# New step costs, hand-over time, array-mode charge and ranks in the planner of a pre-norm attention and slot block

## The chip, the cores and the metric

The kernel runs on one core of a Trainium2 chip, in fp32. The metric is the device time of one execution in microseconds (us): the median of three runs is 686.89, from 686.75 to 687.0. The profile shows one further execution of 686.6 us from the first to the last instruction.

The engines are named as in the profile: PE is TensorE (matmuls; PEld its weight loads), DVE is VectorE, ACT is ScalarE, POOL is GpSimd, SP the queue that issues most of the DMAs. Each engine works through its own queue in the order in which the kernel emitted its instructions; a waiting instruction holds up all behind it on that engine.

## What is computed

For 32 sequences of 512 tokens of width 256 two residual sublayers follow each other:

```
x = x + attn(layernorm(x))
    q     = tanh(x Wc + bc)                      charge, one number a token
    shell = normalised(x Ws + bs)                64 wide
    proj  = shell omega + bias; phi_s = [cos, sin](proj)
    tp    = q**m (m = 0..4)  outer  phi_s        5 x 64
    phi   = tp W_combine                         64 wide
    attn  = softmax(causal(phi phi^T * decay / temp));  out = (attn V) W_out
x = x + slots(layernorm(x))
    h     = gelu([x, mean slot] w1 + b1);  route = (h w2 + b2) / tau
    alpha = softmax over the 8 largest of 64 routes
    gi    = (alpha^T x) / sum(alpha);  S = GRU(gi, S0)
    out   = alpha (S wv + bv) wo
```

## The kernel before

**Groups.** Two sequences (GB = 2, 1,024 tokens, 8 tiles of 128) make a group, so there are 16 groups, g = 0 to 15. Every group goes through the same steps; several groups are under way at once. Names in the program carry the group: pf_3_0 is the projection of tile 0 of group 3.

**One group on PE**, in the order in which data passes, with the name that the profile gives the result and its line:

- pf (L971): a token tile times the fused weights, 128x321. DVE scales it to sv (L984). The transposed tokens xT come by DVE (L941) from blocks that DMAs bring (xb), and in groups 0 and 1 from PE (pta, L919).
- ptq (L1030) and pts (L1101): transposes of the charges (POOL's qrep L1010) and shells (POOL's sq L1057 and rn L1077, DVE's shn L1085); pp (L1118): shells times omega; DVE's turn (L1142), ACT's sine (L1150, with a table load), DVE's products tp (L1164); pph (L1176): tp times W_combine; DVE's phi (L1191).
- pl (L1233): logits; DVE's lg (L1262), ACT's exponential pr (L1274); ptp (L1311): transposes of pr, which ACT copies to prT (L1329); po (L1317): prT times V; DVE adds it to x (L1346). This is done for row tiles (0, 1), 2 and 3 and for both sequences.
- POOL's lnb (L1386), ACT's squares xm (L1398), POOL's deviations (L1412 to L1414), ACT's xm (L1428; DVE in the last two groups, L1424). SP writes xm to DRAM (xd) and reads it back in blocks (xmb), which DVE transposes; in the last two groups PE transposes (ptb, L849) and ACT copies.
- ph (L1458): hidden layer; ACT's gelu h_t (L1467, with a table load); prr (L1481): routes; ACT's rlT (L1495); prt (L1487): transpose; ACT's rl (L1504); DVE's top (L1512), ACT's exponential (L1530), DVE's sums, and alpha al (L1546, POOL; DVE in the last two groups); psi (L1570): alpha^T x.
- pt_gi (L1594), giT (ACT, L1602); prz and pn (L1623): gates; DVE, ACT and POOL steps of the GRU; pt_hn (L1594), hnT (ACT); pv (L1745); DVE's val (L1753); py (L1767): alpha times values; ACT copies it to ys (L1780) and POOL issues an accumulating store (L1807).

**Array modes.** A matmul uses all 128 rows and columns of the array or a part. In the code a PE step carries a split: none for the whole array (pf, po, ph, prz, pn, pv and all transposes), "64x64" for pp and pph, "64x128" for pl and py, "128x64" for prr and psi. The profile shows it as 128*128, 64*64, 64*128 or 128*64.

**Setup.** Weights are folded before group 0: wv times W_out (pw0, pb0), the slot layer's values (pw1, pb1, L452 and L484), the mean slot (pt_hs, pb1 L742), the constant part of the gates (pgh, L775). A bias bv1 is loaded by SP and spread over a tile by DVE (L475).

**The planner.** Nothing is emitted while the steps are described: `add(engine, cost, emit, after, uses, ...)` records a step with its cost in us, what it waits for and which buffers it uses. `Plan.order` then plays the program through, and the steps are emitted in the order in which it placed them. It keeps for each engine the time at which it becomes free, for each kind of buffer the times at which its slots come free, and takes again and again the step with the smallest key (earliest time t at which it can start, rank). A result reaches another engine HOP us after its step's cost. The rank of a step is made of its group times STRIDE, its earliest time within the group, and DELAY of its stage, a pair: the first number counts always, the second times max(0, g - last + 3), that is in the last groups only. A step that would change PE's split has SWITCH added to its rank; no time is charged for the change.

Of the kernel before, what the change touches and what calls it, by code (L numbers as in the profile page):

```python
# [15 lines left out]
P = 128  # L16
# [61 lines left out]
HOP = 0.5  # L78
TABLE = 1.28
SWITCH = 0.23  # L80
STRIDE = 22.39
# [3 lines left out]
    "setup": (0.0, 0.0),  # L85
    "load": (22.2, -11.2),
    "tokens": (0.1, -0.9),
    "angles": (-39.5, -3.6),
    "phi": (-8.7, 0.0),
    "weights": (12.9, -3.8),  # L90
    "values": (-6.4, -1.5),
    "normal": (10.0, -1.9),
    "router": (-0.7, 1.2),
    "taken": (-2.6, 1.8),
    "gru": (28.9, -1.7),
    "given": (43.1, 8.2),
# [25 lines left out]
class Plan:  # L122
# [32 lines left out]
    def order(self):  # L155
# [34 lines left out]
        for n, s in enumerate(self.steps):  # L190
            s.n = n
            if not s.waits:
                ready[s.eng].append(s)
        placed = []
        while len(placed) < len(self.steps):
            best = None
            for e, todo in ready.items():
                for s in todo:
                    t = max(free[e], s.ready)
                    need = {}  # L200
                    ok = True
                    for u in s.uses:
                        if not u.live and u.tag in slots:
                            need[u.tag] = need.get(u.tag, 0) + 1
                    for tag, k in need.items():
                        if len(slots[tag]) < k + (s.spare if tag == "ps" else 0):
                            ok = False
                            break
                        t = max(t, heapq.nsmallest(k, slots[tag])[-1])
                    if not ok:  # L210
                        continue
                    if s.table and s.table != table:
                        key = (t + TABLE, s.rank + TABLE, s.n)
                    elif e == "PE" and s.split != split:
                        key = (t, s.rank + SWITCH, s.n)
                    else:
                        key = (t, s.rank, s.n)
                    if best is None or key < best[0]:
                        best = (key, s, t)
            assert best is not None, "no step can be placed"  # L220
            _, s, t = best
            ready[s.eng].remove(s)
            if s.table and s.table != table:
                t, table = t + TABLE, s.table
            if s.eng == "PE":
                split = s.split
            for u in s.uses:
                if not u.live:
                    u.live = True
                    if u.tag in slots:  # L230
                        heapq.heappop(slots[u.tag])
            s.start, end = t, t + s.cost
            free[s.eng] = end
            for u in s.uses:
                u.left -= 1
                u.end = max(u.end, end + s.land)
                if not u.left and u.tag in slots:
                    heapq.heappush(slots[u.tag], u.end + HOP)
            for o in s.next:
                o.ready = max(o.ready, end + s.land + (HOP if o.eng != s.eng else 0.0))  # L240
                o.waits -= 1
                if not o.waits:
                    ready[o.eng].append(o)
            placed.append(s)
# [4 lines left out]
def block_kernel(ctx: ExitStack, tc: tile.TileContext, a: dict, out: bass.AP):  # L249
# [554 lines left out]
    def statistics(g, src, uses, after):  # L804
# [6 lines left out]
                0.37,  # L811
# [19 lines left out]
        s = add("POOL", 3.3, spread, ss + [s_ones], [st, ts])  # L831
        return ts, s

    def normalised(g, xm, after):
# [4 lines left out]
        for bb in range(GB):  # L839
# [3 lines left out]
            if g >= NG - LAST_BY_TENSOR:  # L843
                for k in range(KD):
                    pt = bank(f"ptb_{g}_{bb}_{k}")

                    def turn(bb=bb, k=k, pt=pt):
                        for c in range(NT):
                            nc.tensor.transpose(  # L849
                                pt()[:, c * P : (c + 1) * P],  # L850
                                xm()[:, bb * NT + c, k * P : (k + 1) * P],
                                ident,
                            )

                    s = add("PE", 0.47, turn, of + [s_ident], [xm, pt, dst])
                    done.append(
                        add(
                            "ACT",
                            0.54,
                            lambda k=k, dst=dst, pt=pt: nc.scalar.copy(dst()[:, k, :], pt()),  # L860
                            [s],
                            [pt, dst],
                        )
                    )
            else:
# [23 lines left out]
                for h in range(2):  # L889
# [12 lines left out]
                    done.append(add("DVE", 0.63, turn, s_b, [xb, dst]))  # L902
# [3 lines left out]
    def columns(g, xt):  # L906
# [3 lines left out]
        for bb in range(GB):  # L910
            dst = lazy("xT", f"xT_{g}_{bb}", [P, KD, T])
            done = []
            if g < BY_TENSOR:
                for k in range(KD):
                    pt = bank(f"pta_{g}_{bb}_{k}")

                    def turn(bb=bb, k=k, pt=pt):
                        for c in range(NT):
# [6 lines left out]
                    s = add("PE", 0.44, turn, [x_in[g][bb], s_ident], [xt, pt, dst])  # L925
# [3 lines left out]
                            0.54,  # L929
# [6 lines left out]
            else:  # L936
                for h in range(2):
# [12 lines left out]
                    done.append([add("DVE", 0.63, turn, xb_in[g, bb], [xbs[g, bb], dst])])  # L950
# [3 lines left out]
    def features(g):  # L954
# [9 lines left out]
        for t in range(GT):  # L964
# [4 lines left out]
            def project(c=c, pf=pf, tile_=tile_):  # L969
                for k in range(KD):  # L970
# [8 lines left out]
            s = add("PE", 1.1, project, done[c // 2] + w_done, [tile_, pf, sv])  # L979
# [3 lines left out]
                    0.42,  # L983
# [44 lines left out]
        def charges_turned():  # L1028
# [7 lines left out]
        s = add("PE", 0.45, charges_turned, s_rep + [s_ident], [qrep, ptq, qs])  # L1036
        s = add(
            "ACT",
            0.61,
# [7 lines left out]
            0.62,  # L1047
# [22 lines left out]
            0.62,  # L1070
# [5 lines left out]
        def norms():  # L1076
# [3 lines left out]
        s_rn = add("POOL", 2.05, norms, [s], [rn])  # L1080
# [3 lines left out]
                0.35,  # L1084
# [20 lines left out]
        s = add("PE", 0.44, shells_turned, s_shn, [shn, pts, sh_t])  # L1105
        s = add("ACT", 0.54, lambda: nc.scalar.copy(sh_t(), pts()), [s], [pts, sh_t])
# [6 lines left out]
        def projected():  # L1113
            for h in range(2):
# [11 lines left out]
        s = add("PE", 0.55, projected, [s, s_om], pps + [sh_t, ang], split="64x64")  # L1126
# [3 lines left out]
                0.41,  # L1130
# [9 lines left out]
        def nearest():  # L1140
# [8 lines left out]
                0.63,  # L1149
# [7 lines left out]
        for m in (1, 3):  # L1157
# [8 lines left out]
            s_tp.append(add("DVE", 1.25, powers, [s_tp[-1], s_q], [tp, qs]))  # L1166
# [4 lines left out]
        def combined():  # L1171
            for m in range(ORDER + 1):
# [12 lines left out]
            "PE", 2.3, combined, s_tp + [s_wc], phs + [tp, phi], split="64x64"  # L1185
# [4 lines left out]
                0.35,  # L1190
# [14 lines left out]
    def attention(g, sv, s_sv, phi, s_phi):  # L1205
# [11 lines left out]
        for tiles in ((0, 1), (2,), (3,)):  # L1217
# [7 lines left out]
            def logits(tiles=tiles, off=off, pls=pls):  # L1225
# [17 lines left out]
                0.15 + width * 0.00167,  # L1243
# [8 lines left out]
            for bb in range(GB):  # L1252
# [3 lines left out]
                for i in tiles:  # L1256
# [16 lines left out]
                    def weights(bb=bb, i=i, c=c, lg=lg, nm=nm, pr=pr, den=den, tiles=tiles):  # L1273
# [10 lines left out]
                        "DVE", 0.11 + 0.12 * (i + 1), lowest, [s_pl, s_mask], [pls[bb], lg, nm]  # L1284
# [4 lines left out]
                            0.31 + 0.105 * (i + 1),  # L1289
# [8 lines left out]
                0.16,  # L1298
# [5 lines left out]
            for bb in range(GB):  # L1304
# [8 lines left out]
                def values(bb=bb, tiles=tiles, off=off, po=po, pr_t=pr_t):  # L1313
# [11 lines left out]
                s = add("PE", 0.119 * width / P, turned, s_ex[bb], [prs[bb], pt, pr_t])  # L1325
                s = add(
                    "ACT",
                    0.18 + 0.09 * width / P,
# [8 lines left out]
                    0.436 * width / P,  # L1337
# [4 lines left out]
                for d, i in enumerate(tiles):  # L1342
# [13 lines left out]
                    s_x[t] = add("DVE", 0.5, added, [s_po, s_den], [po, den, xt, ln])  # L1356
# [17 lines left out]
    def router(g, s_x, ln):  # L1374
# [6 lines left out]
        for tiles in ((0, 1), (2,), (3,)):  # L1381
# [10 lines left out]
            for bb in range(GB):  # L1392
                for i in tiles:
# [3 lines left out]
                            0.6,  # L1397
# [22 lines left out]
        def moved(t):  # L1420
# [6 lines left out]
            else:  # L1427
# [7 lines left out]
                0.25 if by_vector else 0.51,  # L1435
# [15 lines left out]
        for bb in range(GB):  # L1451
# [4 lines left out]
            def hidden(ph=ph, dst=dst):  # L1456
                for k in range(KD):
# [4 lines left out]
            s = add("PE", 1.78, hidden, done + w1_done, [dst, ph, h_t])  # L1462
# [3 lines left out]
                    0.6,  # L1466
# [18 lines left out]
        def routes_turned():  # L1485
# [5 lines left out]
        s = add("PE", 1.01, route, s_h + [l_w2], h_ts + [prr, rl_t], split="128x64")  # L1491
        s = add(
            "ACT",
            0.6,
# [4 lines left out]
        s = add("PE", 0.44, routes_turned, [s], [rl_t, prt, rl])  # L1499
# [3 lines left out]
            0.54,  # L1503
# [5 lines left out]
        for t in range(GT):  # L1509
# [5 lines left out]
            s_top.append(add("DVE", 0.43, taken, [s], [rl, rest, top]))  # L1515
# [4 lines left out]
            0.62,  # L1520
# [8 lines left out]
            0.68,  # L1529
# [6 lines left out]
        def sums():  # L1536
# [4 lines left out]
        s = add("DVE", 1.53, sums, [s], [rl, rest, asum])  # L1541
# [3 lines left out]
                0.7 if by_vector else 1.1,  # L1545
# [12 lines left out]
    def slots(g, xm, al, s_al, stored):  # L1558
# [19 lines left out]
        def amounts():  # L1578
# [3 lines left out]
        s_psi = add("PE", 1.87, taken_in, s_al, [psi, al, xm, gi], split="128x64")  # L1582
        s_gi = add(
            "ACT", 0.38, lambda: nc.scalar.copy(gi(), psi()[:, 0:D]), [s_psi], [psi, gi]
        )
        s_rw = add("DVE", 0.3, amounts, [s_psi], [psi, rw])

        def halves(n, src, s_src):
# [3 lines left out]
            def turn():  # L1592
# [5 lines left out]
            s = add("PE", 0.22, turn, [s_src], [src, pt, dst])  # L1598
            s = add(
                "ACT",  # L1600
                0.38,
# [9 lines left out]
        side, cost = ("DVE", 0.42) if by_vector else ("POOL", 0.73)  # L1611
# [9 lines left out]
        def gates(dst, lo, n):  # L1621
# [9 lines left out]
        s_rz = add("PE", 1.81, lambda: gates(prz, 0, 2 * D), [s] + W_GRU, [gi_t, prz, rz])  # L1631
        s_n = add("PE", 0.86, lambda: gates(pn, 2 * D, D), [s] + W_GRU, [gi_t, pn, nn])
        s = add(
            "DVE",
            0.75,
# [6 lines left out]
            0.6,  # L1642
# [7 lines left out]
            0.42,  # L1650
# [8 lines left out]
            0.38,  # L1659
# [13 lines left out]
        s_nn = add("ACT", 0.42, lambda: nc.scalar.activation(nn(), nn(), AF.Tanh), [s], [nn], "exp")  # L1673
# [12 lines left out]
        s = add("DVE", 0.94, new_state, [s], [rz, rh, nn, hn])  # L1686
# [4 lines left out]
        if g >= NG - LAST_BY_TENSOR:  # L1691
# [10 lines left out]
            s_a = add("PE", 0.58, weights_turned, s_al, [al, pta, al_t])  # L1702
            s_alt = add("ACT", 0.54, lambda: nc.scalar.copy(al_t(), pta()), [s_a], [pta, al_t])
# [39 lines left out]
        def slot_values():  # L1743
# [5 lines left out]
        s = add("PE", 0.86, slot_values, [s] + s_wov, [hn_t, pv, val])  # L1749
        s_val = add(  # L1750
            "DVE",
            0.38,
# [6 lines left out]
        for c2 in range(NT // 2):  # L1759
# [15 lines left out]
            s = add("PE", 0.95, given, [s_val, s_alt], pys + ys + [al_t, val], split="64x128")  # L1775
            for bb in range(GB):
                if stored:
# [6 lines left out]
                    s_ys[bb].append(add("ACT", 0.54, kept, [s], [pys[bb], ys[bb]]))  # L1784
# [17 lines left out]
                s_y = add("DVE", 0.65, added, [s], [pys[bb], xt])  # L1802
# [90 lines left out]
```

## Time and profile before

| | |
|---|---|
| median of 3 runs | 686.89 us |
| profiled execution, span | 686.6 us |
| DVE, ACT, POOL busy | 553.0, 472.2, 253.8 us |
| DMA of the hardware queue q1 | 89.42 MB |
| mean rate of DMA | 153 GB/s |
| costliest PE rows | po 151.1 us, pf 126.1 us, ph 52.0 us |

A row of the profile gives start and duration of an instruction, or of several alike that follow each other (x8), and in brackets how long its engine stood idle before it and what ended the wait. The duration of a matmul runs until its results are out, and the next matmul starts before that; what a step costs PE is therefore read as the distance from its start to the next start. "x" counts matmul records; in fp32 a matmul of the program appears as two records, a transpose as one.

### The profile page before, as it was taken

Reading aid. Unit: us, or ns where it says so; the run is one execution under the profiler, and the core shown is the slowest. Engines: PE = TensorE matmul, PEld = TensorE weight load, DVE = VectorE, ACT = ScalarE, POOL = GpSimd, SP = SyncE. Lnnn points to the kernel's source line nnn. Section 1 sums busy time; section 2 is a strip of 40 time slices with the busy share of each in tenths; the row PEclk is TensorE's granted clock in tenths of the full one; section 3 lists DMA queues with packets and bytes.
Section 4 is the critical chain, followed back from the end, with each engine's and each line's share of the span. In section 5 each row is a group of like instructions: output and inputs, shape, how many; then the busy total and the mean of one; then the engine's idle time right before and its main releaser. Section 6 shows DMA issues by size and latency. Waiting matters only on the chain.

```text
span 686.6 us, 12389 instructions
## 1 busy us (share of the span) xinstructions
PE 658.0 (96%) x3890; PEld 450.4 (66%) x3890; DVE 553.0 (81%) x1770; ACT 472.2 (69%) x1105; POOL 253.8 (37%) x432
## 2 busy tenths in 40 slices
PE   6968999999999999999999999999999999999985
PEld 5646775667666766767666676757666676677553
DVE  5879788989796979979696987879798877877575
ACT  2227777768677777859677785877768686787651
POOL 6420542143525363242535343335334324322221
PEclk9989999999999999999999999999999999999999
DMA  6674377576567596686778594687768518341447
GB/s 186 182 196 121 116 218 189 121 200 132 170 147 154 164 235 176 153 194 144 174 174 183 171 228 131 130 206 174 163 179 168 157 34 184 78 62 32 62 62 184
DMA packets 225362, 105.30 MB, mean 153 GB/s; under 512 B 153360, under 2 KB 224464, under 8 KB 225296
## 3 DMA queue, kind: packets, MB, share of 16 engines
q1 hardware_dynamic: 209344, 89.42, 48.8%
q0 software_dynamic: 15120, 14.98, 15.1%
q8 instruction: 31, 0.51, 0.3%
q14 instruction: 35, 0.29, 0.1%
q10 hardware_dynamic: 832, 0.10, 0.1%
HBM read 54.34 MB, written 49.81 MB: 152 GB/s over the span
## 4 chain that ended last, share of the span: by engine, by line
PE 81%; DVE 5%; DMA 5%; ACT 4%; SPq 2%; issue 1%; POOL 0%; DVEq 0%; ACTq 0%; POOLq 0%
PE po L1317 20%; PE pf L971 16%; PE ph L1458 7%; PE ptp L1311 5%; PE pl L1233 5%; PE pph L1176 4%; PE py L1767 4%; PE psi L1570 4%; PE prz L1623 4%; DMA x<-in_x_dram 2%; SPq L283 2%; PE prr L1481 2%; PE pv L1745 2%; PE pn L1623 2%; PE pp L1118 1%; DMA bv<-in_bv_dram 1%
## 5 line engine op out<-in xcount | busy, mean ns | idle before, releaser
L1317 PE MATMUL po<-sv,prT 128*128 128x256 f32 x640 | 151.1, 381 | 0.7 <-ACT prT L1329 0.7
L1317 PEld LDWEIGHTS po<-sv,prT 128*128 128x128 f32 x640 | 116.0, 189 | 21.4 <-issue 2.9
L971 PE MATMUL pf<-wfb,xT 128*128 128x321 f32 x448 | 126.1, 434 | 0.0
L971 PEld LDWEIGHTS pf<-wfb,xT 128*128 128x128 f32 x448 | 83.6, 190 | 38.3 <-issue 5.3
L984 DVE SCALAR_TENSOR_TENSOR sv<-pf,lna,bias_f 128x321 f32<-128x321 f32 x128 | 64.1, 541 | 17.1 <-PE pf L971 16.9
L1274 ACT ACTIVATE pr<-lg,nm 128x128 f32<-128x128 f32 (+3 forms) x128 | 70.9, 557 | 9.3 <-DVE nm L1262 9.0
L1346 DVE SCALAR_TENSOR_TENSOR x<-po,den,x 128x256 f32<-128x256 f32 x128 | 57.8, 475 | 20.4 <-PE po L1317 19.1
L1398 ACT ACTIVATE xm<-x,lnb 128x256 f32<-128x256 f32 x128 | 63.9, 506 | 8.9 <-POOL lnb L1386 8.5
L1262 DVE CUSTOM_DVE_ANT_0 lg<-pl,mask 128x128 f32<-128x128 f32 (+3 forms) x128 | 56.6, 481 | 6.7 <-PE pl L1233 6.7
L1010 POOL COPY qrep<-sv 128x128 f32<-128x128 f32 x64 | 17.8, 294 | 118.2 <-DVE sv L984 118.2
L1386 POOL TENSOR_SCALAR lnb<-lnb 128x2 f32<-128x2 f32 (+1 forms) x48 | 18.9, 393 | 114.3 <-DVE x L1346 68.8
L1428 ACT ACTIVATE xm<-x,lnb 128x256 f32<-128x256 f32 x112 | 57.3, 590 | 4.3 <-POOL lnb L1414 4.0
L1329 ACT COPY prT<-ptp 128x384 f32<-128x384 f32 (+1 forms) x96 | 46.8, 519 | 18.3 <-PE ptp L1311 17.3
L1807 POOL DMA_DIRECT2D out_dram<-ys x28 | 38.0, 1508 | 47.0 <-ACT ys L1780 45.9
L1458 PE MATMUL ph<-xmT,w1b 128*128 128x512 f32 x112 | 52.0, 595 | 0.5 <-ACT giT L1602 0.5
L812 DVE BATCH_NORM_STATS2 bna<-x 128x6 f32<-128x256 f32 x128 | 46.3, 409 | 1.8 <-DMA x<-in_x_dram 1.8
L1311 PE MATMUL ptp<-ident,pr 128*128 128x128 f32 x320 | 47.1, 278 | 0.2 <-ACT pr L1274 0.2
L1233 PE MATMUL pl<-phi 64*128 64x256 f32 (+1 forms) x384 | 45.2, 361 | 1.3 <-DVE phi L1191 1.3
L1311 PEld LDWEIGHTS ptp<-ident,pr 128*128 128x128 f32 x320 | 36.3, 140 | 15.1 <-ACT pr L1274 4.3
L1164 DVE TENSOR_TENSOR tp<-tp,qs 128x1024 f32<-128x1024 f32 x32 | 39.2, 1226 | 3.5 <-ACT tp L1150 2.8
L1191 DVE TENSOR_TENSOR phi<-pph,dec_q 128x256 f32<-128x256 f32 x32 | 13.4, 418 | 34.7 <-PE pph L1176 34.7
L1233 PEld LDWEIGHTS pl<-phi 64*128 64x128 f32 x384 | 30.8, 186 | 13.3 <-issue 6.5
(178 smaller groups left out, 1309.8 us busy)
## 6 DMA issues: line engine op xcount, KB each, us to landing
x<-in_x_dram SPq DMA_DIRECT2D x32, 512.0 KB, 6.1
xb<-in_x_dram SPq DMA_DIRECT2D x112, 128.0 KB, 3.3
out_dram<-x SPq DMA_DIRECT2D x28, 512.0 KB, 3.7
xd<-xm SPq DMA_DIRECT2D x28, 512.0 KB, 3.3
xmb<-xd SPq DMA_DIRECT2D x112, 128.0 KB, 2.9
out_dram<-ys POOLq DMA_DIRECT2D x28, 512.0 KB, 7.3
ad<-al SPq DMA_DIRECT2D x14, 256.0 KB, 2.4
ab<-ad SPq DMA_DIRECT2D x56, 64.0 KB, 2.7
```

What stands on the lines that cost most here:

```text
L971: nc.tensor.matmul(pf()[:, 0:NF], tile_()[:, k, c * P : (c + 1) * P], w[:, k, :], start=(k == 0), stop=(k == KD - 1),)
L984: lambda t=t, pf=pf: nc.vector.scalar_tensor_tensor(sv()[:, t, :], pf()[:, 0:NF], ln()[:, 1, t : t + 1], bias_f, ALU.mult, ALU.add,),
L1233: nc.tensor.matmul(pls[bb]()[:, off[i] + lo : off[i] + lo + w], phi()[r, 0, q : q + P], phi()[r, 1, k : k + w], start=True, stop=True,)
L1262: nc.vector.tensor_tensor_reduce(out=lg()[:, c], in0=pls[bb]()[:, c], in1=mask[:, T - w : T], scale=1.0, scalar=TOP, op0=ALU.add, op1=ALU.min,
L1274: nc.scalar.activation(pr()[:, c], lg()[:, c], AF.Exp, bias=nm(), scale=-1.0, accum_out=den()[:, tiles.index(i), bb : bb + 1],)
L1311: nc.tensor.transpose(pt()[:, j : j + P], prs[bb]()[:, j : j + P], ident)
L1317: nc.tensor.matmul(po()[:, d * D : (d + 1) * D], pr_t()[:, lo : lo + P], sv()[:, bb * NT + j, C_V:NF], start=(j == 0), stop=(j == i),)
L1329: lambda width=width, pt=pt, pr_t=pr_t: nc.scalar.copy(pr_t()[:, 0:width], pt()[:, 0:width]),
L1346: nc.vector.scalar_tensor_tensor(xt()[:, t, :], po()[:, d * D : (d + 1) * D], den()[:, d, bb : bb + 1], xt()[:, t, :], ALU.mult, ALU.add, ...
L1398: lambda bb=bb, i=i: nc.scalar.activation(xm()[:, bb * NT + i, 0:D], xt()[:, bb * NT + i, :], AF.Square, bias=ln()[:, 2, bb, i : i + 1], a ...
L1428: nc.scalar.activation(xm()[:, t, 0:D], xt()[:, t, :], AF.Identity, bias=bias, scale=scale)
L1458: nc.tensor.matmul(ph(), w1[:, k, :], dst()[:, k, :], start=(k == 0), stop=(k == KD - 1))
```

## The change

Only numbers in the planner and one rule are changed; no step is added, removed or computed differently, and the buffers are the same.

- HOP goes from 0.5 to 0.3.
- A change of PE's split is charged in time: DRAIN 0.094 plus a FILL that depends on the mode entered. Transposes get a split of their own, "turn", which counts as whole array: between None and "turn" nothing is charged.
- SWITCH, the rank added to a step that would change the mode, goes from 0.23 to 1.828.
- STRIDE goes from 22.39 to 22.714, and all pairs of DELAY are new.
- Nearly every cost handed to `add` is new.

```diff
-HOP = 0.5
+HOP = 0.3
+DRAIN = 0.094
+FILL = {None: 0.107, "turn": 0.055, "64x64": 0.054, "128x64": 0.054, "64x128": 0.107}
 TABLE = 1.28
-SWITCH = 0.23
-STRIDE = 22.39
+SWITCH = 1.828
+STRIDE = 22.714
...
-    "load": (22.2, -11.2),
+    "load": (586.66, 41.42),
...
-    "angles": (-39.5, -3.6),
-    "phi": (-8.7, 0.0),
+    "angles": (-254.44, -137.72),
+    "phi": (-94.38, -95.74),
...
-    "given": (43.1, 8.2),
+    "given": (58.48, 52.56),
...
+        def turned_to(s):
+            whole = (None, "turn")
+            if s.split == split or (s.split in whole and split in whole):
+                return 0.0
+            return DRAIN + FILL[s.split]
...
-                    elif e == "PE" and s.split != split:
-                        key = (t, s.rank + SWITCH, s.n)
+                    elif e == "PE":
+                        lag = turned_to(s)
+                        key = (t, s.rank + (SWITCH if lag else 0.0), s.n)
...
             if s.eng == "PE":
+                t += turned_to(s)
                 split = s.split
...
-            s = add("PE", 1.1, project, done[c // 2] + w_done, [tile_, pf, sv])
+            s = add("PE", 1.082, project, done[c // 2] + w_done, [tile_, pf, sv])
...
-                s = add("PE", 0.119 * width / P, turned, s_ex[bb], [prs[bb], pt, pr_t])
+                s = add("PE", 0.109 * width / P, turned, s_ex[bb], [prs[bb], pt, pr_t], split="turn")
                 s = add(
                     "ACT",
-                    0.18 + 0.09 * width / P,
+                    0.05 + 0.107 * width / P,
...
-                    0.436 * width / P,
+                    0.432 * width / P,
...
-        s = add("PE", 1.01, route, s_h + [l_w2], h_ts + [prr, rl_t], split="128x64")
+        s = add("PE", 0.865, route, s_h + [l_w2], h_ts + [prr, rl_t], split="128x64")
         s = add(
             "ACT",
-            0.6,
+            0.57,
...
-        s_psi = add("PE", 1.87, taken_in, s_al, [psi, al, xm, gi], split="128x64")
+        s_psi = add("PE", 1.74, taken_in, s_al, [psi, al, xm, gi], split="128x64")
...
-            s = add("PE", 0.95, given, [s_val, s_alt], pys + ys + [al_t, val], split="64x128")
+            s = add("PE", 0.863, given, [s_val, s_alt], pys + ys + [al_t, val], split="64x128")
```

The built program has the same 2,270 matmuls and transposes; what changes is their order, and that of the instructions on the other engines. Lines of the changed kernel are 12 higher than those of the kernel before, from the costs on; the text names lines of the kernel before.

## The prediction

> **What bounds the kernel now.** I read the busy shares first, then the same by stretch, then what PE waits for at both ends, last the chain of waits. Busy shares of the page:
>
> ```profile
> PE 658.0 (96%) x3890; PEld 450.4 (66%) x3890; DVE 553.0 (81%) x1770; ACT 472.2 (69%) x1105; POOL 253.8 (37%) x432
> ```
>
> By stretch (length, PE, PEld, DVE, ACT, POOL busy, clock, DMA share, GB/s):
>
> ```profile
> 0.00:62.00 62.00, 46.95 (x281) 33.12 (x282) 44.66 (x117) 22.30 (x42) 23.58 (x56) 0.94 0.71 189
> 62.00:162.00 100.00, 97.73 (x564) 69.09 (x564) 86.35 (x282) 72.88 (x184) 35.78 (x73) 1.00 0.56 152
> 162.00:644.00 482.00, 482.00 (x2870) 328.87 (x2869) 394.58 (x1282) 358.59 (x845) 187.89 (x297) 1.00 0.66 152
> 644.00:681.00 37.00, 31.36 (x180) 19.33 (x178) 25.74 (x90) 18.41 (x37) 6.60 (x6) 1.00 0.61 105
> ```
>
> From 162 to 644 us PE is never idle, and DVE, the next, is at 82%. So three sums can move: what PE issues in the middle, its idle time in the head, and the chain after the last attention matmul.
>
> What a change of array mode costs is in PE's timeline (start, duration, step):
>
> ```profile
> 345.28 1.03 PE L1623 MATMUL pn<-wih,giT 128*128 128x256 f32 x4
> 346.14 0.38 PE L1594 MATMUL pt_hn<-ident,hn 128*128 128x128 f32 x2
> ...
> 347.31 0.66 PE L1030 MATMUL ptq<-ident,qrep 128*128 128x128 f32 x4
> 347.90 0.92 PE L1233 MATMUL pl<-phi 64*128 64x256 f32 x8
> 348.75 1.13 PE L1745 MATMUL pv<-wov,hnT 128*128 128x256 f32 x4
> 349.81 1.14 PE L1233 MATMUL pl<-phi 64*128 64x256 f32 x8
> ...
> 355.24 0.60 PE L1101 MATMUL pts<-ident,shn 128*128 128x128 f32 x4
> 355.68 2.54 PE L1317 MATMUL po<-sv,prT 128*128 128x256 f32 x11
> ```
>
> Read starts. Four matmuls of 256 columns take PE 346.14 - 345.28 = 0.86 among steps of their own mode (pn), and 349.81 - 348.75 = 1.06 between two pl (pv): one entry and one exit cost 0.20. Four transposes take 0.44 among whole-array steps (pts) and 0.59 between two pl (ptq): 0.15. So a change costs 0.15 to 0.20.
>
> In the head DVE and PE wait for one small transfer (brackets: idle before, and for what):
>
> ```profile
> 45.80 0.48 DVE L475 TENSOR_SCALAR setup<-onesP,bv 128x128 f32<-128x128 f32 x2 [4.46 <-DMA bv<-in_bv_dram]
> ```
>
> ```profile
> 47.09 1.09 PE L1101 MATMUL pts<-ident,shn 128*128 128x128 f32 x4 [4.45 <-DVE shn L1085]
> ```
>
> **The middle.** I counted mode changes in the instruction order of both built programs: 215 before, 168 after. The 47 removed enter transposes (20), other whole-array steps (7) and pl or py (20). At 0.15, 0.20 and 0.20 that is 3.0 + 1.4 + 4.0 = 8.4 us; bounds 47 x 0.15 = 7.1 and 47 x 0.20 = 9.4. Of it 8.0 lies before the last po, 0.4 behind. Cause: the two py of a group now follow pl and psi follows py, and pv and ptq no longer cut pl apart, so a period has 9 changes, against 12 to 17 before. To trust such sums I added, for each stretch between successive pph of the old order, matmuls times their distance in the trace plus the changes: 39.3 where the trace has 39.2, 40.0 where it has 39.9, and so on for 10 stretches. The new order gives 38.8 for each of groups 6 to 11, so 38.7 on the chip.
>
> The Trainium skill, TensorEngine Tiling, Key Properties, says that changing the tiling mode drains TensorE; its TensorE: Matmul & The Clock Gate, Step-by-step, puts a drain at about 128 cycles of 2.4 GHz, an estimate of 0.053 us. By the page the 47 changes would be worth 2.5 us, by the rows 8.4.
>
> Do the shorter hand-overs open waits in PE? I compared, step by step, how much PE work lies between a result and the step that needs it. Two places got clearly tighter. (a) prr to prt: 2.4 us before, now one pf tile, 1.08. At 642.31 prr starts, at 643.32 the next step, at 643.46 rlT on ACT, and prt follows a rlT that it waited for by 0.72 (653.12, 653.84): need 0.14 + 0.72 = 0.86, so 0.2 is left. (b) pph of the next group starts 3.43 (ph) + 1.08 (pf) = 4.5 after the last po, before 6.7. Its chain on ACT: prT is copied 4.1 before po's end, six squares of 0.49, a table load 1.28, the sine 0.54, so 0.7 after it; then DVE's two products, 2.44, with 0.15 to 0.2 a hand-over: 3.5. So 1.0 is left. Elsewhere the distance is at or above one that did not stall before, or twice its bare chain: ptp to po 1.3 against 0.2 + 0.37 + 0.15; psi to pt_gi 1.6 against 0.65. Queued behind rlT are ACT's xm and the copy rl; top on DVE waits for that, with 14 us of PE work before psi, as before. POOL's two accumulating stores (1.37 and 1.28 at 395.68 and 398.08) move ahead of rh (L1677); what waits there, hn, has 36.9 us of PE work before pt_hn. SP issues the same transfers; xmb and ab swap places, and ph keeps 38.8 us behind po (least before: 31.2). I book nothing for all this; bounds 0 and 0.3 a period at (a), 4 us over 13.
>
> **The head.** To 25.5 us the order is the same. Then group 0's pts, pp, turn, tp and pph stand ahead of the rest of group 1. By rows: hs, statistics, rn on DVE to 29; xT of group 2, whose blocks land at 29.92; shn to 31.2; pts 31.4, pp 32.7; decay scalars, three transposes and three sv before turn (35.5 to 36.6); sine, then three sv, a copy and tp, 41.3; pph at 41.5, not 51.9. SP's queue is unchanged there, so bv still lands at 45.8; its wait is now in front of phi: spread 0.28 and four phi of 0.33 end at 47.4, pl starts at 47.5, not 55.4. PE rows and changes before that pl sum to 32.3, in the old order to 35.1: time lost 15.2 against 20.3. Onward by pr, prT, a table load, the sine and tp, group 1's pph starts at 61.3 with 44.9 of PE rows done, before 58.4 with 37.5: 16.4 lost against 20.9. I take 4.5 gained. From there to 155 us the old order lost 3.4 more in short waits; I give the new one the same. Bounds of the gain: 0, if every step in this walk is 4.5 late, and 7, if those waits shrink too. PE's idle gap before pph is about 4.6; after the gap of 4.45 the next rows ran slow (pts 1.09, not 0.60) and cost some 2 us in all, which here falls into time in which PE waits for bv anyway; without that cover, 2.
>
> **The tail.** From the end of the last po, 633.1, to the end are 53.5 us. 1.3 us of PE work (half of py 11, four transposes ptb) now comes before that po: +1.3 ahead of it. Behind it prt of group 14 stands 1.5 earlier, and its exponential is what holds ACT before rlT of 15 (653.12); py 13 no longer stands between psi and pt_gi of 15. I followed this to 0.8 at psi and 2.2 at prz of 15 and take 1.5; bounds 0 (all hidden in DVE's and ACT's chain) and 3.
>
> **Sum.** 686.6 - 8.0 + 1.3 - 4.5 - 1.5 = 673.9. The median stands 0.3 above the profiled span, so 674.2.
>
> **Rivals.**
> 1. The head gives nothing: another landing (x of group 2, freed by gh_n) holds DVE as bv did. For it: DVE has bna before tp of group 1. Against: gh_n is computed some 2 us earlier. 674.2 + 4.5 = 678.7.
> 2. Short waits in the middle: at (a) ACT is late every period, by up to 0.8. For it: rlT was often behind two squares. Against: by the chain above those are done 3 us earlier. 13 x 0.6 = 8: 682.
> 3. Slower: at (b) POOL holds lnb, so squares 5 and 6, the sine and pph come late. For it: POOL took 1.01 for lnb at 365.16, beside two stores of 2.68. Against: the stores are moved away from there. The 12.7 us won are eaten when pph waits 1.06 in each of 12 periods, which is a chain 2.1 late; at 2.7 late it waits 1.7, 20 us: 694.
> That the planner does not do what it says is excluded: the changes are counted.
>
> **How the numbers follow.** Forecast (671 to 677) 0.60, still faster 0.05, first rival 0.20, second 0.07, slower 0.06, about as before 0.02. Faster is the sum of the first four, 0.92. A difference under 0.2% (1.4 us) is no change here. The bounds downwards are head 2.5, tail 1.5 and changes 1.0; they will not all fall together: 669.5. Upwards the range takes in the first rival and half of the second: 681.
>
> **What would show it.** pph starts 38.7 apart in groups 6 to 11, with no idle PE between 160 and 640. In a period 9 mode changes, no ptq or pv between two pl. First pph near 41.5, first pl at 47.5 behind bv. Last po ends near 621.5 with some 52 behind it. Wrong if prt or pph shows idle time every period, if the first pl comes after 52, or if the end keeps its 53.5.

## The result, and the profile after

The changed kernel is slower, where 674.2 us had been forecast: 705.36 us (703.86 to 708.2, 4 runs) against 686.94 us in the same comparison, a ratio of 1.0269 (95% interval 1.0237 to 1.0300). Its profiled execution spans 701.9 us. Busy shares of its page, then the stretches (length, PE, PEld, DVE, ACT, POOL busy, clock, DMA share, GB/s):

```profile
PE 661.8 (94%) x3890; PEld 452.3 (64%) x3890; DVE 558.6 (80%) x1770; ACT 468.2 (67%) x1106; POOL 256.1 (36%) x432
```

```profile
0.00:62.00 62.00, 52.41 (x318) 37.27 (x319) 49.16 (x138) 25.59 (x56) 23.74 (x58) 1.00 0.70 189
62.00:162.00 100.00, 97.28 (x559) 67.94 (x558) 85.89 (x278) 73.31 (x181) 36.59 (x73) 0.98 0.59 158
162.00:644.00 482.00, 464.86 (x2765) 316.42 (x2764) 387.67 (x1239) 339.60 (x808) 186.26 (x289) 1.00 0.66 151
```

The head is better, as foreseen. The loss is in the middle: from 162 to 644 us PE, which had been busy all 482 us, is idle for 17, and does not get through its work. (The idle time is not all of the loss. Over groups 6 to 11 the changed kernel has 236 matmul records a period, as has e11, the last of the experiments below. It takes 41.7 us for them, 1.8 of these idle; e11 takes 38.9 with no idle time. So another 1.0 us a period sits in rows that count as busy.) Set against the landmarks of the prediction (us; "middle" is the distance between the first pph of successive groups, mean of groups 6 to 11; the last column is the best run of the experiments):

| | before | predicted | changed | e11 |
|---|---|---|---|---|
| first pph starts | 51.9 | 41.5 | 39.9 | 40.2 |
| first pl starts | 55.4 | 47.5 | 45.6 | 45.3 |
| second pph starts | 58.4 | 61.3 | 59.3 | 59.0 |
| middle | 39.6 | 38.7 | 41.7 | 38.9 |
| last po ends | 633.1 | 621.5 | 651.1 | 621.1 |
| from there to the end | 53.5 | 52 | 50.8 | 50.8 |
| span | 686.6 | 673.9 | 701.9 | 671.9 |

One line is off, the middle, by 3 us in each period. The four largest waits of PE there, from 300 to 520 us (us in total, times, longest):

```profile
PE py L1779 <- DVE val L1765: 3.3, 6, 0.6
PE psi L1582 <- DVE nm L1274: 2.7, 5, 0.5
PE prt L1499 <- ACT rlT L1507: 1.7, 5, 0.3
PE ptq L1042 <- POOL qrep L1022: 1.1, 6, 0.2
```

Many short waits at several places, every period the same: something goes round. The chain of waits of the changed kernel shows what. One turn of it (start, duration, piece):

```profile
330.46 0.44 DVE x L1358 x2
330.90 0.68 DVE bna L824 x2
...
334.94 1.67 POOL lna L841
336.61 0.22 POOL lnb L1398
...
338.31 1.67 POOL lnb L1425
...
340.29 1.59 ACT xm L1440 x3
341.87 0.47 ACT rl L1516
...
346.76 2.38 DVE sv L996 x5
...
355.71 1.81 DVE xT L953 x3
...
362.37 6.97 DMA xmb<-xd
...
369.46 0.58 DVE xmT L905
...
372.16 0.38 DVE x L1358 x2
```

From x at 330.46 to the same x of the next group at 372.16 are 41.7 us, and no PE step is in it. DVE's x feeds bna, POOL's lna of a later group stands in front of lnb, ACT's squares and three xm stand in front of rl, DVE's top and all that is queued behind it stand in front of xT, xT gives back the buffer that SP needs for xmb, and DVE waits for the last block of xmb with the next x behind it:

```profile
369.46 0.71 DVE L905 STREAM_TRANSPOSE xmT<-xmb 128x512 f32<-128x512 f32 x1 [2.48 <-DMA xmb<-xd]
```

From 162 us to the last po the chain of before was PE alone; now PE follows a loop of the other queues.

The longest single piece is a transfer of 6.97 us. The issues around it, in the kernel before (two rows of SP, one of POOL) and in the changed one:

```profile
351.82 1.92 SPq L883 DMA_DIRECT2D xmb<-xd  x4
...
356.22 1.90 SPq L883 DMA_DIRECT2D xmb<-xd  x4
```

```profile
363.21 2.68 POOL L1807 DMA_DIRECT2D out_dram<-ys  x2 [3.51 <-ACT ys L1780]
```

```profile
356.37 7.51 SPq L895 DMA_DIRECT2D xmb<-xd  x8
```

```profile
356.38 2.70 POOL L1819 DMA_DIRECT2D out_dram<-ys  x2
```

Before, POOL's two accumulating stores started 7 us after the second four blocks of xmb. Now they start in the same instant as the first block. Eight issues take 7.51 us of SP instead of 1.92 and 1.90, and the page's row for these 128 KB blocks (median us from issue to landing) goes from 2.9 to 6.1:

```profile
xmb<-xd SPq DMA_DIRECT2D x112, 128.0 KB, 2.9
```

```profile
xmb<-xd SPq DMA_DIRECT2D x112, 128.0 KB, 6.1
```

### The profile page after: what moved, and what is told of

Read it like the earlier page. It is cut to its first block, busy times and chain, and to the rows that moved or that the text cites. A ratio compares the mean times of both kernels' runs of the same rounds, so it can differ in the third digit from the quotient of the medians.

```text
span 701.9 us, 12354 instructions
## 1 busy us (share of the span) xinstructions
PE 661.8 (94%) x3890; PEld 452.3 (64%) x3890; DVE 558.6 (80%) x1770; ACT 468.2 (67%) x1106; POOL 256.1 (36%) x432
## 4 chain that ended last, share of the span: by engine, by line
PE 36%; DVE 25%; SPq 9%; DMA 9%; POOL 8%; ACT 7%; issue 4%; DVEq 0%; ACTq 0%; POOLq 0%
PE po L1329 10%; PE pf L983 8%; SPq L895 4%; DVE rest L1525 4%; DMA xmb<-xd 3%; SPq L1735 3%; PE ph L1470 3%; DVE sv L996 3%; PE ptp L1323 3%; DVE xT L953 3%; PE pl L1245 2%; POOL lna L841 2%; DVE top L1524 2%; POOL lnb L1425 2%; SPq L295 2%
## 5 line engine op out<-in xcount | busy, mean ns | idle before, releaser
L1329 PE MATMUL po<-sv,prT 128*128 128x256 f32 x640 | 148.5, 382 | 0.0
L983 PE MATMUL pf<-wfb,xT 128*128 128x321 f32 x448 | 130.3, 439 | 0.0
L1329 PEld LDWEIGHTS po<-sv,prT 128*128 128x128 f32 x640 | 117.9, 191 | 17.7 <-ACT prT L1341 1.2
L983 PEld LDWEIGHTS pf<-wfb,xT 128*128 128x128 f32 x448 | 83.6, 192 | 45.3 <-issue 15.7
L1398 POOL TENSOR_SCALAR lnb<-lnb 128x2 f32<-128x2 f32 (+1 forms) x48 | 13.1, 273 | 161.1 <-DVE x L1358 142.2
L905 DVE STREAM_TRANSPOSE xmT<-xmb 128x512 f32<-128x512 f32 x56 | 37.3, 692 | 22.2 <-DMA xmb<-xd 22.1
L1245 PE MATMUL pl<-phi 64*128 64x256 f32 (+1 forms) x384 | 44.2, 359 | 2.0 <-DVE phi L1203 2.0
L1524 DVE MAX8 top<-rl 128x8 f32<-128x64 f32 x128 | 28.0, 219 | 19.8 <-ACT rl L1516 19.8
```

The lines of the kernel that those rows point to most:

```text
L983: nc.tensor.matmul(pf()[:, 0:NF], tile_()[:, k, c * P : (c + 1) * P], w[:, k, :], start=(k == 0), stop=(k == KD - 1),)
L1245: nc.tensor.matmul(pls[bb]()[:, off[i] + lo : off[i] + lo + w], phi()[r, 0, q : q + P], phi()[r, 1, k : k + w], start=True, stop=True,)
L1329: nc.tensor.matmul(po()[:, d * D : (d + 1) * D], pr_t()[:, lo : lo + P], sv()[:, bb * NT + j, C_V:NF], start=(j == 0), stop=(j == i),)
```

## The experiments

All start from the changed kernel unless said otherwise, and keep its PE order unless said. Ratios are to the kernel before.

| run | time us | ratio (95%) | middle |
|---|---|---|---|
| changed | 705.36 | 1.0269 (1.0237 to 1.0300) | 41.7 |
| e1 stores later | 682.02 | 0.9909 (0.9882 to 0.9936) | 39.3 |
| e2 lna later | 684.66 | 0.9964 (0.9949 to 0.9979) | 39.5 |
| e3 third xb | 684.75 | 0.9954 (0.9937 to 0.9971) | 39.5 |
| e4 no stores | 678.65 | 0.9873 (0.9853 to 0.9893) | 39.3 |
| e5 = e1 + e2 | 679.08 | 0.9896 (0.9880 to 0.9913) | 39.2 |
| e6 = e5, bv early | 678.07 | 0.9877 (0.9859 to 0.9894) | 39.2 |
| e7 = e5, ptq between pl | 680.52 | 0.9920 (0.9894 to 0.9946) | 39.2 |
| e8 old ranks, new costs | 723.26 | 1.0543 (1.0522 to 1.0564) | 34 to 46 |
| e9 new ranks, old costs | 735.03 | 1.0698 (1.0654 to 1.0741) | 34 to 50 |
| e10 = e6, rn later | 677.88 | 0.9871 (0.9851 to 0.9891) | 39.2 |
| e11 = e10, xT later | 675.44 | 0.9840 (0.9824 to 0.9855) | 38.9 |

**Cutting the loop at one place.** Four kernels, each with one link changed in the list that the planner hands back:

```diff
             placed.append(s)
+        for s in [s for s in placed if s.emit.__name__ == "accumulate"]:
+            k = placed.index(s)
+            for j in range(k + 1, min(len(placed), k + 200)):
+                if placed[j].eng == "POOL" and placed[j].stage == "normal":
+                    placed.insert(j, placed.pop(k))
+                    break
         return placed
```

> The changed kernel with one edit: in POOL's queue both accumulating stores of a group are moved behind the next lnb step, so they start some 9 us after the first block of xmb is issued instead of together with it. Theory collision: the stores slow the read-back (the later blocks of xmb land 6 to 10 us after issue in the changed kernel, 2.2 to 3.7 in the kernel before, where the stores start 9 us later or at the last block), DVE waits for the last block with x behind it, and the loop x, lna, lnb, xm, rl, al, xT, xmb takes 41.7 us instead of PE's 38.8. Then blocks land 2 to 4 us after issue, groups 6 to 13 follow at 38.8 +- 0.2, the waits of PE before prt, py and psi go, and the time falls by ten times 2.9: 673 to 678 us. Theory lna (POOL's lna of the later group stands in front of lnb and holds squares, rlT and prt): POOL's order of lna and lnb is as it was, so period 41.5 and 700 to 706 us. Theory hand-overs (0.3 is too short, all engines packed too tightly): as lna, within 3 us of 704.

For e2 the same loop moves the POOL step "spread" (lna) behind "deviations" (lnb):

```diff
+        for s in [s for s in placed if s.emit.__name__ == "spread" and s.eng == "POOL"]:
...
+                if placed[j].emit.__name__ == "deviations":
+                    placed.insert(j, placed.pop(k))
```

> The changed kernel with one edit: lna (4.9 us of POOL in the changed kernel's rows) is moved behind the three steps of lnb that follow it. Theory lna: lnb, the last two squares and rlT come up to 2 us earlier (ACT is then free at 376.5 instead of being held to 378.5), the waits before prt go and the period falls to about 39.5: 682 to 688 us. Theory collision: the loop keeps its transfer and its DVE order; DVE and SP take up what ACT wins only in part: 41.0 to 41.8 a period, 697 to 706 us. Theory hand-overs: 700 to 706.

```diff
-                tc.tile_pool(name=f"{tag}_pool", bufs=SLOTS_OF.setdefault(tag, 1), **kind)
+                tc.tile_pool(name=f"{tag}_pool", bufs=SLOTS_OF.setdefault(tag, 1) + (tag == "xb"), **kind)
```

> The changed kernel with a third buffer for xb, which xmb and the blocks of the input share, the order of all queues unchanged. The read-back need no longer wait for DVE's xT and can be issued as soon as xm is written, some 8 us earlier (348 instead of 356). Theory collision: most blocks land before the stores start; the loop loses the wait for the slot, but the input blocks now meet the stores: period 38.8 to 40.3, 676 to 691 us. Theory lna: 41.5 a period, 700 to 706. Theory hand-overs: the same.

```diff
         for s in plan.order():
-            s.emit()
+            if s.emit.__name__ != "accumulate":
+                s.emit()
```

> The changed kernel without the 28 accumulating stores: the slot layer's contribution to groups 0 to 13 is left out of the output, all else is computed in the same order. POOL is spared 2.7 us a group and DMA the traffic of 512 KB read and written per store. Theory collision: the same period as with the stores moved, 38.8, blocks of xmb land 2 to 4 us after issue, 671 to 677 us. If it was POOL's 2.7 us in front of rh and not the traffic, this run falls as much, but the run with the stores moved would show blocks that still land after 6 to 9 us. Theories lna and hand-overs: 698 to 706.

All four came out fast, and so both of my theories were too narrow: "collision" expected e2 to stay near 700, "lna" expected e1 to. "Collision" also promised more than came: 38.8 a period, with 673 to 678 us in e1 and 671 to 677 in e4. In e1 the stores start 9 us behind the first block of xmb, and the blocks are quick again (SP's and POOL's rows, then the page's):

```profile
351.14 4.08 SPq L901 DMA_DIRECT2D xmb<-xd  x8
```

```profile
360.44 2.68 POOL L1825 DMA_DIRECT2D out_dram<-ys  x2
```

```profile
xmb<-xd SPq DMA_DIRECT2D x112, 128.0 KB, 2.9
```

Moving the stores was enough, though POOL still spends 2.7 us on them, and leaving them out (e4) gave the same 39.3. Nor is it that they hold up POOL's rh for 2.7 us: from 162 to 644 us of the changed kernel DVE waited for that rh 0.2 us in all. So it is their traffic in the same moment as the read-back. In e2 the blocks are as slow as in the changed kernel and the middle still falls to 39.5: POOL's order was a link of the same loop, and a loop is cut at any link.

```profile
xmb<-xd SPq DMA_DIRECT2D x112, 128.0 KB, 6.2
```

In e3 most blocks are issued ahead of the stores and only the last two or four are slow (median of all 3.1). "Hand-overs" falls in all four: HOP is 0.3 in each.

**What is left, and what a mode change costs.** All cuts ended at 39.3 to 39.5, above the 38.8 that PE's rows sum to. e5 has both edits of POOL's queue. e6 also issues the load of bv1 first among the setup loads. e7 is e5 with one PE step moved. `behind(name, last)` is the loop of e1 in general form: it moves the steps of that name behind the next step for which `last` is true.

```diff
+        behind("accumulate", lambda s, o: o.eng == "POOL" and o.stage == "normal")
+        behind("spread", lambda s, o: o.emit.__name__ == "deviations")
...
+        l_bv.early = n == 1
...
+        behind("charges_turned", lambda s, o: o.emit.__name__ == "logits" and o.g == s.g - 1, 25)
```

> The changed kernel with both edits of POOL's queue: the accumulating stores behind lnb and lna behind the three steps of lnb. Theory loop: one chain goes round once a period without PE, x, bna, lna, lnb, squares, lnb, xm, rl, top, al, xT, xmb, xmT, x; each edit alone took it from 41.7 to about 39.2 to 39.5, just above PE's own 38.8, and both together take it well below. Then groups 6 to 11 follow at 38.8 +- 0.1 with no wait of PE before psi, 0.4 less in each of 10 periods than with the stores moved: 674 to 679 us. Theory floor: the 39.2 is what PE needs (the changes of array mode cost more than the rows said): 39.2 again, 679 to 684 us.

> As with both edits, and the small load of bv1 is the first of the setup loads in SP's queue (issued near 15 us instead of 37.5, so it lands some 20 us earlier). Theory clock: PE's idle 2 to 4 us in front of the first pl is what lets the granted clock fall to 0.66 between 45 and 55 us in the kernel before and in some executions after; without the wait for bv the first pl starts at 43 to 44 instead of 45 to 46, the clock stays at 1.00 there in every execution, and the time falls by 2 to 4 us against the run with both edits, with less spread. Theory absorbed: whatever is won before 60 us is waited for at the shells of group 3 near 110 us, where ACT and DVE end last: first pl earlier, last po unchanged, within 1 us of the run with both edits.

> As with both edits, and in 9 groups the four transposes ptq are moved behind the first row tile of pl, as the kernel before had them. It adds two changes of array mode a period, 186 in all against 168, and no work. By the rows of before (pl to transposes 0.15, transposes to pl 0.20) a period grows by 0.35, from 38.8 to 39.15, and the time by 3.2 us; by the rule of the Trainium skill (a drain of about 128 cycles at 2.4 GHz, 0.053 us for each change) by 0.11 a period and 1 us in all. Theory nothing: the changes cost nothing and the gain of the new order lies elsewhere: no growth.

e5 still has 39.2, with one wait of PE left, before psi. Its PE timeline, and that of e7 at the same place:

```profile
340.82 1.03 PE L1648 MATMUL pn<-wih,giT 128*128 128x256 f32 x4
341.69 0.60 PE L1055 MATMUL ptq<-ident,qrep 128*128 128x128 f32 x4
342.22 1.58 PE L1258 MATMUL pl<-phi 64*128 64x128 f32 x16
343.63 1.90 PE L1792 MATMUL py<-val,alT 64*128 64x256 f32 x16
345.74 1.96 PE L1595 MATMUL psi<-xm,al 128*64 128x257 f32 x16 [0.21 <-DVE nm L1287]
```

```profile
340.44 1.03 PE L1649 MATMUL pn<-wih,giT 128*128 128x256 f32 x4
341.40 0.93 PE L1259 MATMUL pl<-phi 64*128 64x128 f32 x8
342.26 0.66 PE L1056 MATMUL ptq<-ident,qrep 128*128 128x128 f32 x4
342.84 0.92 PE L1259 MATMUL pl<-phi 64*128 64x256 f32 x8
343.60 1.90 PE L1793 MATMUL py<-val,alT 64*128 64x256 f32 x16
```

The same matmuls from pn to py take 343.63 - 340.82 = 2.81 in e5 and 343.60 - 340.44 = 3.16 in e7: two more changes of mode cost 0.35, as the rows of before said. By the Trainium skill (TensorEngine Tiling (Array Packing), Key Properties, with the drain of TensorE: Matmul & The Clock Gate, Step-by-step) two drains of about 128 cycles would come to 0.11 us, an estimate from its figures; the measurement decides. But e7's period is the same 39.2: the 0.35 went into the wait before psi, which is gone there. That told me that 39.2 was not PE's, so "floor" falls too: a second loop was just above PE.

The early bv1 took DVE's wait for it away, and the first pl still started at 45.0, as in e5: DVE's steps in front of phi end at 44.2 either way. The median fell by 1.0 us, with overlapping intervals; neither "clock" nor "absorbed" is settled by that.

**The second loop.** e10 moves one DVE step, e11 another:

```diff
+        behind(
+            "<lambda>",
+            lambda s, o: o.emit.__name__ == "lowest" and o.g < s.g,
...
+            lambda s: s.stage == "angles" and s.cost == 0.6,
+        )
```

> As with both edits of POOL's queue and the early load of bv1, and DVE's sum for rn (0.6 us) is moved behind the first lg step that follows it. In the run with both edits the period stayed at 39.2, and it stayed there with 0.35 us more of PE work too, so it is not PE's own. Theory bank: psi takes the bank of PSUM that pl of the first row tile gives back, and DVE gives it back only after lg (345.58, psi starts at 345.74); ACT, DVE and PE then go round from prr over rlT, rl, top, alpha and lg to psi and back to prr in 39.2. The first lg pair then ends 0.6 us earlier, psi does not wait, groups 6 to 11 follow at 38.8, and 10 periods bring 4 us: 673 to 675.5 us. Theory alpha: psi waits for al, which this edit leaves where it is: 39.2 a period and 677 to 679 us.

In e10 the wait before psi went, and reappeared a few steps on. Its PE timeline:

```profile
345.76 0.55 PE L1349 MATMUL ptp<-ident,pr 128*128 128x128 f32 x3
346.28 0.44 PE L1632 MATMUL pt_gi<-ident,gi 128*128 128x128 f32 x2
346.82 0.63 PE L1139 MATMUL pts<-ident,shn 128*128 128x128 f32 x4
```

From ptp to the next start are 0.52 and from pt_gi 0.54, where the two take 0.38 and 0.34 in the changed order when nothing holds them (e11, below): pt_gi waits for gi, pts for shn. So "bank" was right about the place and wrong about the loop: the period did not move. "Alpha" had the right time, 677 to 679 us, for a wrong reason: psi no longer waits, though al was left where it is. What both waits share is DVE, which in e5 works without a break from its top (rl arrives at 332.7) through sv, xT, rz, alpha, val, rh, lg and xT. e11 takes 0.6 us more out of the way:

```diff
+            xts = [s for s in on[max(0, q - 5) : q] if s.emit.__name__ == "turn" and s.stage == "tokens"]
+            shn = [s for s in on[q : q + 4] if s.stage == "angles" and s.cost == 0.31]
...
+            if shn[1] in rest:
+                placed[lo : hi + 1] = rest + held
```

> As the run with DVE's rn moved, and the last of the three xT that DVE does in front of rw and shn is moved behind shn (0.6 us). That run took the wait before psi away, but the period stayed at 39.2: pt_gi (behind gi, which waits for rw) and pts (behind shn) now wait 0.2 and 0.3. Theory stretch: the loop is DVE's unbroken run of work from rl to shn, and whatever PE step first needs its end waits; rw and shn then come 0.6 earlier, the waits of pt_gi and pts go, groups 6 to 11 follow at 38.8: 673 to 675.5 us. Theory next link: the waits move on once more, to po, whose banks DVE's later lg steps give back: 39.0 to 39.3, 675.5 to 678.5 us.

The period fell to 38.9, as "stretch" expected; PE is busy from 162 us to the last po, and the chain of waits is PE alone there again. The stretch of e11, and its timeline at the same place:

```profile
162.00:621.00 459.00, 458.98 (x2792) 319.77 (x2791) 388.12 (x1247) 341.55 (x816) 171.72 (x290) 1.00 0.68 158
```

```profile
345.20 0.55 PE L1363 MATMUL ptp<-ident,pr 128*128 128x128 f32 x3
345.58 0.38 PE L1646 MATMUL pt_gi<-ident,gi 128*128 128x128 f32 x2
345.92 0.63 PE L1153 MATMUL pts<-ident,shn 128*128 128x128 f32 x4
```

e11 beats both kernels: 675.44 us, 1.6% under the one before (ratio 0.9840, 0.9824 to 0.9855) and some 30 us under the changed one, with the same steps, costs and ranks and the same order on PE, matmul for matmul; five steps of each period are moved on the other queues, and one load of the setup.

**The parts of the change alone.** e8 has the new costs, hand-overs and mode charge with the old DELAY, STRIDE and SWITCH; e9 is the kernel before with the new ones of these three.

> One part of the change alone: the measured costs, the shorter hand-overs and the time charged for a mode change, but DELAY, STRIDE and SWITCH as before. 192 changes of array mode, 23 fewer than before. Theory parts: each part brings its share, here 23 changes at 0.18, 4 us: 681 to 685 us. Theory together: the ranks of before were fitted to the costs of before and no longer space the stages well with the new ones; PE waits for DVE, ACT and transfers in every period: 700 to 730 us.

> The other part of the change alone: the costs, hand-over time and free mode changes of before, with the new DELAY, STRIDE and SWITCH. 214 changes of array mode, as many as before. Theory parts: no mode changes saved, so within 2 us of the kernel before (685 to 689), or a little less by the earlier first pl. Theory together: the new ranks fit only the new costs; with the old ones the stages drift apart and PE waits: 700 to 730 us.

Both are far slower than the two together, as "together" expected, e9 even beyond its 730 us. From 162 to 644 us PE idles 11 us in e8, at pts, prt, po and psi, and 18 in e9, most of it at pts, pp and pv; blocks of xmb land after 4.1 and 3.6 us (medians). Part of the time is a lower mean clock, 0.977 and 0.972 in these two profiles against 0.994 in that of the changed kernel. In these runs neither half does without the other: the ranks fit the costs with which they were chosen, so no part of the change can be credited or blamed by itself. The shorter HOP and the charge for a mode change were not run alone.

## Why the prediction was wrong

**The failed step** is in the part on the middle: "Elsewhere the distance is at or above one that did not stall before, or twice its bare chain", after which I booked nothing, with bounds of 0 and 0.3 a period. I measured each hand-over in PE work between a result and the step that needs it. That catches a link that is too short on its own. It cannot catch a loop through the other engines, where each link looks as long as before because every one of them is late by the same amount. The loop was 41.7 us, so the term was 3.0 a period, not 0. (The prediction's own sign of being wrong, idle time at prt, is there: five waits in the 220 us above.) Over ten periods that is the 29.6 us by which the last po ends later than forecast; the tail gave 1.2 of it back.

**The two sentences that had it in hand.** "POOL's two accumulating stores ... move ahead of rh" and "SP issues the same transfers; xmb and ab swap places". For the stores I asked who stands behind them in POOL's queue, and found hn with 36.9 us of room. I did not ask what runs in the DMA engines at the moment to which they move. It was the read-back, with DVE waiting for it. A shared resource without a queue of its own in the code has to be followed like a queue.

**The check of the sums** (39.3 against 39.2 in the trace) was made on an order in which PE never waited. It proves the prices, not that the new order has no waits. Three slips in the working cost little. The terms put the last po at 633.1 - 8.0 + 1.3 - 4.5 = 621.9, not 621.5. "One entry and one exit cost 0.20" reads a distance from start to start that holds one change only; the sum did use 0.15 to 0.20 for each change, and e7's pair of 0.35 agrees with that. And the 0.3 us between the median and the profiled span come from two executions: in one and the same the time is some 2 us above the span (704.0 and 701.9), so the profile of before was of an execution slower than the median.

**The rivals.** The second (ACT late at prt, up to 0.8 a period) named a place where PE then did wait, with the right witness, rlT behind two squares, but as a delay of ACT's own worth 8 us. The third asked for a pph chain 2.7 late and put POOL's lnb in it; lnb was late, but its price came round the loop and not at pph, where PE waits 0.1 to 0.2. Its "the stores are moved away from there" was meant as an argument for safety, and that move is what slowed the read-back.

**What held.** The mode changes: 0.35 for a pair measured in e7; 38.9 a period in e11, where nothing else holds PE, against 38.7 forecast. The head: with the rows and changes priced as in the prediction, PE's time lost before group 4's shells, at 152 us, is 19.5 in the changed kernel, as forecast (16.4 + 3.4 = 19.8), and 24.3 before. It was 2 us better than forecast until 60 us, and gave that back in front of the shells of group 3, near 110 us, where PE idles 2.5 us and the clock then falls (0.91 between 105 and 125 us). The end: 50.8 behind the last po, forecast 52. In e11, with the loops opened, the last po ends at 621.1 (forecast 621.5) and the time is 675.4 (forecast 674.2). The medians are the fairer measure, since e11's profile is of the fastest of its five executions: 11.3 us won, where 12.7 were forecast. The forecast was near the time of the PE order; the other queues of that order did not allow it.

## What to carry to other kernels

When a schedule is tightened around its bound engine, walk once round every loop of the other queues over one period (engine order, buffers, DMA landings) and compare its length with the new period; a list of links with slack does not show it. Ask of every moved transfer what else is in flight where it lands, and plan with the landing time that it has there. When such a loop binds, it can be cut at its cheapest link, which need not be the one that grew; and a wait that moves on instead of vanishing says that the next loop is the limit, not the engine that waits.

## What the runs showed of the hardware

- Two accumulating stores of 512 KB from POOL's queue, started together with eight blocks of 128 KB on SP's, made the third block and those behind it land after 6 to 10 us, where blocks land after 2 to 3 in the middle of the kernel before and of e1. From the sixth block on they also stretched SP's own issues from 0.5 to between 0.8 and 2.5 us. The Trainium skill (DMA: Bandwidth & Descriptors, Queues, rings and completion order) says that a DMA engine takes turns between the queues that have work, a packet at a time; the rows agree that queues are not separate roads.
- POOL's small steps and DVE's can hold each other up. In the changed kernel the steps L839 and L840 of lna have medians of 0.20; at 374.23 and 375.32 us they took 1.00 and 1.17, each until one of DVE's two tp products (373.95 to 376.4) ended. So lna, 3.17 us in the planner, took 5.0 in the loop. The other way round, DVE's rh took 0.99 at 352.54 instead of 0.42, beside POOL's al (352.21 to 353.25). The Trainium skill (GPSIMD Engine Reference, Specifications) lists the SBUF interfaces as shared with VectorE, with contention for DVE instructions that have two SBUF inputs or run in a 2-port mode; in the rows tp and rh have two inputs each.
- The granted clock differs between executions. Between 45 and 55 us it was 0.66 in the profiles of before, e1 and e3, 0.83 in e4, e5 and e9, and 1.00 in the changed kernel and the others; between 105 and 125 us it was 0.91 in the changed kernel, e1 to e5 and e7, and 1.00 in before, e6 and e8 to e11. In before it was 0.50 from 45 to 51 us, and the rows that the prediction calls slow after the gap (pts 1.09, not 0.60) are in that stretch. The four executions of the changed kernel follow their mean clock: 703.9 and 704.0 us at 0.996 and 0.994, 706.7 and 708.2 at 0.991 and 0.989. What decides it in a given execution was not settled.
